# Part of the next image's sampling moved from the attention loop to the stage before it

## The chip, the cores and the metric

The kernel runs on one NeuronCore of a Trainium2 chip. A core has five engines that run side by side, each in the order of its own instructions: PE (TensorE, matrix products; its weight loads are listed apart as PEld), DVE (VectorE, elementwise work and reductions), ACT (ScalarE, activation functions), POOL (GpSimd, elementwise work and indirect transfers) and SP (SyncE, which issues most transfers). They wait for one another by semaphores. The metric is the device time of one execution in microseconds (us); the median of the runs shown is given, and less is better.

## The reference

The input is a batch of four images of 64 x 64 positions with 256 channels, that is 4096 tokens an image, all in float32. Two layers follow each other.

```
# layer 0: x = x + DCN(group_norm(x))
xp     = x @ in_w + in_b
x1     = silu(batch_norm(depthwise_conv3x3(x)))
offset = x1 @ off_w + off_b                     # 8 groups x 9 points x 2
mask   = softmax(x1 @ mask_w + mask_b over the 9 points)
out    = sum over points of mask * bilinear_sample(pad(xp), position + offset)
x      = x + out @ out_w + out_b

# layer 1, on tokens t of one image
v      = layer_norm(t)
q, k   = v @ Wt, v @ Wx.T                       # 32 units each
alpha  = sum_u tanh(q_u + k_u + bh_u) * Wa_u    # 4096 x 4096
t      = t + softmax(alpha) @ v
n      = layer_norm(t)
w      = n @ wr                                 # one weight a token
sel    = the 2047 tokens of largest w
y      = 0, but y[sel] = w[sel] * (gelu(n[sel] @ w1 + b1) @ w2 + b2)
t      = t + n + y
```

## The kernel before

The kernel works in stages. A first stage computes, for all four images, the projection `xp`, the offsets and the masks, and stores them. Then the sampling of image 0 runs alone. After that comes, for each image n, a *stage* and an *attention loop*. In the stage the feed-forward of image n-1 (`feed_forward`) and the attention preparation of image n (`attention_prep`) run interleaved. In the loop the attention of image n runs, and beside it the sampling of image n+1 (`sample_image`). Loop 3 has no sampling beside it. At the end the feed-forward of image 3 runs alone.

**The attention loop** (`attention`) has 8 query blocks by 32 key blocks, that is 256 tiles. The order of the work in a tile is written out by hand in four lists, one for each of ACT, PE, DVE and POOL (`order`), each entry with a lag in tiles, and `emit` issues them when what they need is done. In a tile PE makes six products `d` (line 869) and six products `nn` (line 879); ACT takes logarithm and exponential of three pairs of `d` (lines 951 and 953); DVE multiplies each of the six halves with its `nn` (line 884, entries `m1a` to `m3b`), POOL adds three of them (lines 957 and 959), DVE makes two more additions (lines 961 and 964), ACT the weight exponential (line 890). Every eight tiles give values to add up by eight products a tile on PE (line 906, `gather_values`); DVE adds them to the sums (`hand_over`). There are two PSUM buffers for `d`, three for `nn`, and one, "pm", for the values and for everything that the sampling needs from PE; `S.bank` says whether it is free.

**The sampling** (`sample_image`) is a Python generator: each `next` emits one step. First `list_tokens` makes the list of the tokens whose offsets are larger than one (32 one-hot comparisons at line 548, each with a product on PE). Then, for each of four chunks of 1024 positions and two channel halves, come 25 window positions. Each loads 512 KB of weights `wb` (line 673, on SP), multiplies (line 682, writing `prd`) and, but for the first, adds (line 689); each of the two is one step. So an image has 200 multiplications and 192 additions. After a chunk, four output steps each make four products with `outwp` (line 701), two DVE additions (lines 705 and 708) and a store. `wb` has two buffers in the loops. `single` is a second generator inside it, `exact_rows`, which gathers the listed tokens' samples exactly by 144 indirect transfers on POOL (line 616) and multiplies and reduces them on DVE (lines 627 and 628); it is advanced by one step after every multiplication.

In the loop the sampling is advanced by the entry `side`, which stands twice in DVE's list, so two steps a tile, until it is exhausted:

```
[("m1a", 1), ("m1b", 1), ("m2a", 1), ("side", 0), ("s3b", 2), ("side", 1), ("m2b", 1), ("sum", 2),
 ("m3a", 1), ("m3b", 1), ("out", 3)],
```

**The stage** advances its two generators by a string of turns, `m` for the feed-forward and `o` for the preparation. The feed-forward finds the threshold of the 2047 largest weights digit by digit (`kth_largest`), writes the rows in order of selection to DRAM by 32 indirect transfers on POOL (`sort<-v`, line 1253), stores the normalised rows (`base`, line 1266 on ACT, the store on SP), and then works through four groups of 512 rows: row load `xs` (line 1277, SP), normalisation on ACT (1286), transposes on PE and eviction `xT` on DVE (763, 764), hidden layer on PE (1302) and gelu on ACT, output layer on PE (1307), addition on DVE into `vs`, indirect store on POOL (1314). The preparation loads and normalises the tokens and then goes through eight *units*: transposes and eviction `vT`, products `pq` (795), threshold at zero `mm` (802), products `pk` and `pf` (810, 816), two exponentials on ACT (811, 818), the minimum `least` on DVE (828), a store of the query factor on SP (819).

Instructions that go through `keep` hold the order in which they are emitted; `pinned` does that for all DVE instructions of a function. The others are placed by a scheduler. Tiles come from pools; the names in `scope` give pool, buffers a tag, and whether it lies in PSUM.

Of the kernel before, what the change touches and what calls it, by code (L numbers as in the profile page):

```python
# [16 lines left out]
P = 128  # L17
# [14 lines left out]
CH = 1024  # L32
U = 32
# [11 lines left out]
def layers_kernel(ctx: ExitStack, tc: tile.TileContext, a, out: bass.AP):  # L45
# [185 lines left out]
    S = SimpleNamespace(bank=True, wants=False)  # L231
# [298 lines left out]
    def list_tokens(n):  # L530
# [22 lines left out]
        uf = S.two.tile([P, 1], F32, tag="uf", name="uf")  # L553
# [5 lines left out]
    def exact_rows(n, uf, out_rows):  # L559

        ui = S.two.tile([P, 1], I32, tag="ui", name="ui")
        nc.vector.tensor_copy(ui, uf)
        rf = S.two.tile([P, 1], F32, tag="rf", name="rf")
        nc.vector.tensor_scalar(rf, uf, float(L - 1), None, ALU.min)
        ri = S.two.tile([P, 4], I32, tag="rii", name="rii")
# [5 lines left out]
        hw = S.two.tile([P, 2], F32, tag="hw", name="hw")  # L571
# [72 lines left out]
        tt = S.sb.tile([P, C], F32, tag="tte", name="tte")  # L644
# [9 lines left out]
    def sample_image(n, depth=1):  # L654
# [8 lines left out]
        for c in range(L // CH):  # L663
            ac = S.dn.tile([P, CC, CH], F32, tag="ac", name="ac", bufs=min(depth, 2))
            for f in range(CC):
# [5 lines left out]
                for d in range(ND):  # L671
# [14 lines left out]
                    next(single, None)  # L686
# [4 lines left out]
            for i in range(0, CH // P, 2):  # L691
                while bank_taken():
                    next(single, None)
                    yield
# [22 lines left out]
    def sample_any(n):  # L717

        num = nc.values_load(large[0:1, n : n + 1], min_val=0, max_val=L)
        with tc.If(num > P), scope(  # L720
            ("two", 2, 0), ("sb", 2, 0), ("dn", 1, 0), ("ps_t", 1, 1), ("ps_m", 1, 1)
# [44 lines left out]
    def attention_prep(n, v, kf, vec):  # L766
# [33 lines left out]
        def below_zero(s):  # L800
            mms[s] = S.sb.tile([P, 512], F32, tag="mm", name="mm")
            vec.tensor_scalar(mms[s], pqs.pop(s), bqk, 0.0, ALU.add, ALU.min)

        def products(s):
# [14 lines left out]
            nc.sync.dma_start(out=qf_d[n][:, :, o], in_=qe)  # L819
# [4 lines left out]
        for s in range(8):  # L824
            if s < 7:
                units(s + 1)
            products(s)
            vec.tensor_reduce(least[:, s : s + 1], pks.pop(s).rearrange("p b q -> p (b q)"), AX.X, ALU.min)
            if s < 7:
                below_zero(s + 1)  # L830
            yield
# [12 lines left out]
    def attention(n, v, kf, beside):  # L844
# [94 lines left out]
        nb = NQ * NT  # L939
        rs, ds, ns = {}, {}, {}  # L940

        def emit(op, b):
# [31 lines left out]
            elif op == "side":  # L974
                for side in beside:
                    next(side, None)
# [5 lines left out]
            [("m1a", 1), ("m1b", 1), ("m2a", 1), ("side", 0), ("s3b", 2), ("side", 1), ("m2b", 1), ("sum", 2),  # L982
# [219 lines left out]
    def feed_forward(n, vec):  # L1202
# [60 lines left out]
        for i in range(NT):  # L1263
            if i % 4 == 0:
                base = S.sb.tile([P, 4, C], F32, tag="base", name="base")
            nc.scalar.activation(  # L1266
                base[:, i % 4, :], v[:, i, :C], AF.Identity, bias=nm[:, i : i + 1], scale=r1[:, i : i + 1]
            )
            if i % 4 == 3:
                nc.sync.dma_start(  # L1270
                    out=out_d[n, (i - 3) * P : (i + 1) * P].rearrange("(t p) c -> p t c", p=P), in_=base
                )
        yield
        hT2 = S.one.tile([P, 2, FF // P, 512], F32, tag="big", name="hT")
        for s in range(NSORT // 512):
            xs = S.row.tile([P, 4, C + 4], F32, tag="xs", name="xs")
            get = nc.sync.dma_start(  # L1277
# [26 lines left out]
            for t in range(4):  # L1304
# [12 lines left out]
                )  # L1317

# [18 lines left out]
    with scope(("two", 2, 0), ("sb", 2, 0), ("dn", 1, 0), ("ps_m", 2, 1)):  # L1337
# [3 lines left out]
    for n in range(NB):  # L1341
        with scope(("att", 1, 0)):
            v = S.att.tile([P, NT, C + 1], F32, name="v")
            kf = S.att.tile([P, 2, L], F32, name="kf")
            with scope(
# [3 lines left out]
                if n == 0:  # L1349
                    for _ in attention_prep(n, v, kf, nc.vector):  # L1350
                        pass
                else:


                    main, other = feed_forward(n - 1, pinned), attention_prep(n, v, kf, pinned)
                    for turn in "ommm" + "mo" * 5 + "moooo" + "moooo" + "m" + "mo" * 4:
                        next(main if turn == "m" else other, None)
                    for rest in (main, other):
                        for _ in rest:
                            pass  # L1360
            with scope(
                ("two", 2, 0), ("sb", 2, 0), ("dn", 1, 0), ("rp", 6, 0), ("qp", 2, 0),
                ("ep", 2 * PVB + 1, 0), ("ap", 1, 0), ("ps_d", 2, 1), ("ps_n", 3, 1), ("ps_m", 1, 1),
            ):
                attention(n, v, kf, [sample_image(n + 1)] if n + 1 < NB else [])
# [42 lines left out]
```

## Time and profile before

| | us |
|---|---|
| median of 3 runs | 11087.07 (11078.03 to 11089.36) |
| the profiled execution | 11100.44, span 11098.7 |
| PE busy in the span | 9437.4 (85%) |
| DVE busy | 8666.5 (78%) |
| ACT busy | 7403.1 (67%) |
| POOL busy | 5060.5 (46%) |
| mean granted PE clock | 0.896 |

The page lists the costliest groups of instructions: line, engine, operation, written and read tiles, form and count, then the busy time in us with the mean of one in ns, and the engine's idle time ahead of them with what ended most of it. The rows of the loop and of the sampling:

```profile
L879 PE MATMUL nn<-qn,kf 32*128 32x512 f32 (+1 forms) x12288 | 4727.3, 656 | 317.0 <-DVE r L884 272.6
L884 DVE TENSOR_TENSOR r<-nn,r 128x512 f32<-128x512 f32 x6144 | 3941.4, 682 | 1036.1 <-PE nn L879 1012.6
L957 POOL TENSOR_TENSOR r<-r 128x1024 f32<-128x1024 f32 x1024 | 2722.5, 2659 | 3347.2 <-DVE r L884 3345.0
L951 ACT ACTIVATE r<-d 128x1024 f32<-128x1024 f32 x3072 | 3120.4, 1016 | 1648.2 <-DVE r L961 1042.3
...
L689 DVE TENSOR_TENSOR ac<-ac,prd 128x1024 f32<-128x1024 f32 x768 | 1008.6, 1313 | 6.2
L682 DVE TENSOR_TENSOR prd<-xs,wb 128x1024 f32<-128x1024 f32 x768 | 984.2, 1282 | 0.0
L616 POOL DMA_INDIRECT ga<-tab,tii x576 | 731.8, 1270 | 241.3 <-issue 121.3
```

Each row sums over all four images. An average over the span mixes the loops with the stages between them, whose busy engines are not the same; windows of the span, each with the busy time of every engine in it, keep them apart. In the span, stage 0 lies at 1475 to 1569 us, loop 0 from there to 3730, the second stage to 4054, loop 1 to 6211, the third stage to 6522, loop 2 to 8679, the fourth stage to 8986, loop 3 to 10870, and the last feed-forward to the end.

### The profile page before, as it was taken

Reading aid. Unit: us, or ns where it says so; the run is one execution under the profiler, and the core shown is the slowest. Engines: PE = TensorE matmul, PEld = TensorE weight load, DVE = VectorE, ACT = ScalarE, POOL = GpSimd, SP = SyncE. Lnnn points to the kernel's source line nnn. Section 1 sums busy time; section 2 is a strip of 40 time slices with the busy share of each in tenths; the row PEclk is TensorE's granted clock in tenths of the full one; section 3 lists DMA queues with packets and bytes.
Section 4 is the critical chain, followed back from the end, with each engine's and each line's share of the span. In section 5 each row is a group of like instructions: output and inputs, shape, how many; then the busy total and the mean of one; then the engine's idle time right before and its main releaser. Section 6 shows DMA issues by size and latency. Waiting matters only on the chain. (4 is left out here: it accounts for less than half of the span.)

```text
span 11098.7 us, 116284 instructions
## 1 busy us (share of the span) xinstructions
PE 9437.4 (85%) x38460; PEld 4569.9 (41%) x38460; DVE 8666.5 (78%) x13502; ACT 7403.1 (67%) x8395; POOL 5060.5 (46%) x2931
## 2 busy tenths in 40 slices
PE   7870059999999689999999689999999699999996
PEld 4540024444444344444444344444444344444444
DVE  7767879898998549899998559899997457777772
ACT  4440037777878547777878457777878478888882
POOL 0005126654445337654545336654545245555552
PEclk9985569899999889899999889899999899999998
DMA  3336633222221223222220223322220200000002
GB/s 114 122 129 197 215 103 76 67 73 66 75 72 33 82 60 76 67 76 67 71 72 28 86 62 77 66 72 71 71 73 20 89 19 6 9 9 7 7 5 73
DMA packets 380819, 766.01 MB, mean 69 GB/s; under 512 B 48592, under 2 KB 212080, under 8 KB 380176
## 3 DMA queue, kind: packets, MB, share of 16 engines
q1 hardware_dynamic: 350032, 712.34, 19.8%
q0 software_dynamic: 30144, 45.87, 2.9%
q8 instruction: 309, 5.06, 0.2%
q14 instruction: 334, 2.74, 0.1%
HBM read 580.88 MB, written 177.14 MB: 68 GB/s over the span
## 5 line engine op out<-in xcount | busy, mean ns | idle before, releaser
L879 PE MATMUL nn<-qn,kf 32*128 32x512 f32 (+1 forms) x12288 | 4727.3, 656 | 317.0 <-DVE r L884 272.6
L884 DVE TENSOR_TENSOR r<-nn,r 128x512 f32<-128x512 f32 x6144 | 3941.4, 682 | 1036.1 <-PE nn L879 1012.6
L957 POOL TENSOR_TENSOR r<-r 128x1024 f32<-128x1024 f32 x1024 | 2722.5, 2659 | 3347.2 <-DVE r L884 3345.0
L951 ACT ACTIVATE r<-d 128x1024 f32<-128x1024 f32 x3072 | 3120.4, 1016 | 1648.2 <-DVE r L961 1042.3
L869 PE MATMUL d<-qf,kf 32*128 32x512 f32 (+1 forms) x12288 | 3431.6, 647 | 57.3 <-ACT r L951 49.3
L953 ACT ACTIVATE r<-r 128x1024 f32<-128x1024 f32 x3072 | 3125.3, 1051 | 32.6
L879 PEld LDWEIGHTS nn<-qn,kf 32*128 32x128 f32 (+1 forms) x12288 | 1456.7, 189 | 2196.5 <-DVE r L884 1755.7
L906 PE MATMUL pv<-v,et 128*128 128x257 f32 x8192 | 2258.8, 422 | 14.9 <-DVE acv L926 14.9
L906 PEld LDWEIGHTS pv<-v,et 128*128 128x128 f32 x8192 | 1606.2, 206 | 1079.2 <-issue 835.1
L869 PEld LDWEIGHTS d<-qf,kf 32*128 32x128 f32 (+1 forms) x12288 | 1034.0, 189 | 1328.1 <-issue 636.0
L959 POOL TENSOR_TENSOR r<-r 128x512 f32<-128x512 f32 x1024 | 1322.5, 1292 | 163.5 <-DVE r L884 88.9
L689 DVE TENSOR_TENSOR ac<-ac,prd 128x1024 f32<-128x1024 f32 x768 | 1008.6, 1313 | 6.2
L682 DVE TENSOR_TENSOR prd<-xs,wb 128x1024 f32<-128x1024 f32 x768 | 984.2, 1282 | 0.0
L616 POOL DMA_INDIRECT ga<-tab,tii x576 | 731.8, 1270 | 241.3 <-issue 121.3
L890 ACT ACTIVATE et<-et,nshift 128x512 f32<-128x512 f32 x1024 | 725.3, 708 | 25.1 <-DVE et L964 25.1
L961 DVE TENSOR_TENSOR r<-r 128x512 f32<-128x512 f32 x1024 | 712.4, 696 | 13.3 <-POOL r L957 12.9
L964 DVE TENSOR_TENSOR et<-r 128x512 f32<-128x512 f32 x1024 | 696.1, 680 | 6.0 <-POOL r L959 5.6
L701 PE MATMUL pmo<-outwp,ac 128*128 128x256 f32 x512 | 138.9, 421 | 455.7 <-DVE ac L689 407.6
L115 ACT ACT_TABLE_LOAD x9 | 11.5, 1283 | 768.6 <-DVE mv L743 681.8
L476 POOL MEMSET w<- 128x1600 f32 x16 | 22.9, 1433 | 675.1 <-PE ptw L493 388.1
L701 PEld LDWEIGHTS pmo<-outwp,ac 128*128 128x128 f32 x512 | 100.9, 206 | 513.0 <-DVE ac L689 284.8
L416 PE MATMUL pc<-xn,diag 128*128 128x512 f32 x576 | 263.0, 611 | 33.4 <-ACT xn L362 33.4
(354 smaller groups left out, 5211.1 us busy)
## 6 DMA issues: line engine op xcount, KB each, us to landing
wb<-wt SPq DMA_DIRECT2D x800, 512.0 KB
tab<-tb SPq DMA_DIRECT2D x128, 256.0 KB
v<-t SPq DMA_DIRECT2D x64, 512.0 KB
xs<-xp SPq DMA_DIRECT2D x32, 680.0 KB
xp<-xp SPq DMA_DIRECT2D x32, 544.0 KB
xt<-in_x_dram SPq DMA_DIRECT2D x32, 512.0 KB
xr<-in_x_dram SPq DMA_DIRECT2D x64, 256.0 KB
t<-xr SPq DMA_DIRECT2D x64, 256.0 KB
```

The source lines that it names most:

```text
L616: keep(nc.gpsimd.indirect_dma_start(out=ga[:, s, dy].rearrange("p c e -> p (c e)"), out_offset=None, in_=tab_d[n], in_offset=bass.Indirect ...
L682: keep(nc.vector.tensor_tensor(pr.rearrange("p (r w) -> p r w", w=W), src, wb.rearrange("p (r w) -> p r w", w=W), ALU.mult,))
L689: keep(nc.vector.tensor_add(ac[:, f, :], ac[:, f, :], pr))
L869: keep(nc.tensor.matmul(d[:, j, :], kf[g, blk, rows(kt)], qs[q][0][g, blk, :], start=True, stop=True))
L879: keep(nc.tensor.matmul(nn, kf[g, blk, rows(kt)], qs[q][1][g, blk, :], start=True, stop=True))
L884: keep(nc.vector.tensor_tensor(r[:, j, :], ns[j], r[:, j, :], ALU.mult))
L890: keep(nc.scalar.activation(ets[b], ets[b], AF.Exp, bias=nshift))
L906: keep(nc.tensor.matmul(pv, ets[b0 + i][:, rows(j)], v[:, k0 + i, :], start=(i == 0), stop=(i == PVB - 1)))
L951: keep(nc.scalar.activation(rs[b, p], ds.pop((b, p)), AF.Ln))
L953: keep(nc.scalar.activation(rs[b, p], rs[b, p], AF.Exp, scale=-1.0))
L957: keep(nc.gpsimd.tensor_tensor(rs[b, 1], rs[b, 1], rs[b, 2], ALU.add))
L959: keep(nc.gpsimd.tensor_tensor(rs[b, 1][:, 0], rs[b, 1][:, 0], rs[b, 3][:, 0], ALU.add))
```

## The change

The sampling of image n+1 is begun in the stage before loop n. The string of turns gets a third letter, `s`, for one step of sampling. Stage 0 takes 26 such steps, the later stages 122; what is left goes on in the loop. There one step a tile is taken, and a second one (`again`) in as many tiles as the rest of 412 steps needs: 130 of 256 in loop 0, 34 in loops 1 and 2. While the stage runs, `S.gather` is false, and the multiplications don't advance the exact rows.

So that both fit and don't queue behind one another, other things change. The sampling's small tiles get a pool `smp`, and `dn` now lives over stage and loop. `mm` has one buffer instead of two. `base` holds two row blocks instead of four, with three buffers, and is stored from ACT's queue; the query factors too. The row loads `xs` are issued on POOL instead of SP. The feed-forward yields after each of the first three output products of a group, the preparation twice more in each unit, so that steps can be set between them. Stage 0 runs the preparation pinned.

```diff
@@
-    S = SimpleNamespace(bank=True, wants=False)
+    S = SimpleNamespace(bank=True, wants=False, gather=True)
@@ sample_image
-                    next(single, None)
+                    if S.gather:
+                        next(single, None)
                     yield
@@ attention_prep
-            mms[s] = S.sb.tile([P, 512], F32, tag="mm", name="mm")
+            mms[s] = S.sb.tile([P, 512], F32, tag="mm", name="mm", bufs=1)
...
-            nc.sync.dma_start(out=qf_d[n][:, :, o], in_=qe)
+            nc.scalar.dma_start(out=qf_d[n][:, :, o], in_=qe)
...
             if s < 7:
                 units(s + 1)
+            yield
             products(s)
             vec.tensor_reduce(least[:, s : s + 1], pks.pop(s).rearrange("p b q -> p (b q)"), AX.X, ALU.min)
+            yield
             if s < 7:
                 below_zero(s + 1)
             yield
@@ attention
-    def attention(n, v, kf, beside):
+    def attention(n, v, kf, beside, steps):
...
+        second = min(max(steps - nb, 0), nb)
...
-            elif op == "side":
+            elif op == "side" or op == "again" and (b + 1) * second // nb > b * second // nb:
                 for side in beside:
                     next(side, None)
...
-            [("m1a", 1), ("m1b", 1), ("m2a", 1), ("side", 0), ("s3b", 2), ("side", 1), ("m2b", 1), ("sum", 2),
+            [("m1a", 1), ("m1b", 1), ("m2a", 1), ("side", 0), ("s3b", 2), ("again", 1), ("m2b", 1), ("sum", 2),
@@ feed_forward
-            if i % 4 == 0:
-                base = S.sb.tile([P, 4, C], F32, tag="base", name="base")
+            if i % 2 == 0:
+                base = S.sb.tile([P, 2, C], F32, tag="base", name="base", bufs=3)
...
-                nc.sync.dma_start(
-                    out=out_d[n, (i - 3) * P : (i + 1) * P].rearrange("(t p) c -> p t c", p=P), in_=base
+                nc.scalar.dma_start(
+                    out=out_d[n, (i - 1) * P : (i + 1) * P].rearrange("(t p) c -> p t c", p=P), in_=base
...
-            get = nc.sync.dma_start(
+            get = nc.gpsimd.dma_start(
                 out=xs, in_=sort_d[n][s * 512 : (s + 1) * 512].rearrange("(t p) c -> p t c", p=P)
...
+                if t < 3:
+                    yield
@@ layers_kernel
-        with scope(("att", 1, 0)):
+        with scope(("att", 1, 0), ("smp", 2, 0), ("dn", 1, 0)):
...
+            sampling = sample_image(n + 1) if n + 1 < NB else iter(())
+            S.gather = False
...
-                    for turn in "ommm" + "mo" * 5 + "moooo" + "moooo" + "m" + "mo" * 4:
-                        next(main if turn == "m" else other, None)
+                main = feed_forward(n - 1, pinned) if n else iter(())
+                prep = attention_prep(n, v, kf, pinned)
+                if n:
+                    turns = "ommm" + "mo" * 5 + "moooo" + "mss" + "oss" * 12 + "m" + ("ossss" * 3 + "msss" * 4) * 4
+                else:
+                    turns = "o" * 10 + "ss" + "os" * 24
+                for turn in turns:
+                    next({"m": main, "o": prep, "s": sampling}[turn], None)
...
+            S.gather = True
...
-                attention(n, v, kf, [sample_image(n + 1)] if n + 1 < NB else [])
+                attention(n, v, kf, [sampling], STEPS - turns.count("s") if n + 1 < NB else 0)
```

`STEPS` is 412.

## The prediction

> **What bounds the kernel now.** I read the page's slices first, then a window for each stage and loop, then the waits inside the loops, then the stage by time. The slices say where to cut:
>
> ```profile
> DVE  7767879898998549899998559899997457777772
> ...
> PEclk9985569899999889899999889899999899999998
> ```
>
> The first three attention loops have VectorE (DVE) at 8 to 9 tenths, the fourth at 7; between loops DVE falls to 4 or 5. The windows put sizes on that (us, busy time and instructions of PE, weight loads, DVE, ACT, POOL, then granted clock, DMA share, GB/s):
>
> ```profile
> 1475.00:1569.00 94.00, 62.47 (x161) 26.77 (x162) 41.64 (x95) 34.57 (x51) 0.16 (x1) 0.76 0.28 95
> 1569.00:3730.00 2161.00, 2036.83 (x8370) 943.06 (x8371) 1938.00 (x2891) 1655.85 (x1794) 1195.66 (x659) 0.93 0.22 63
> 3730.00:4054.00 324.00, 215.37 (x672) 128.84 (x670) 98.31 (x310) 100.44 (x147) 57.48 (x53) 0.77 0.30 96
> 4054.00:6211.00 2157.00, 2032.74 (x8354) 937.80 (x8355) 1933.11 (x2864) 1653.83 (x1792) 1197.16 (x659) 0.94 0.22 63
> 8986.00:10870.00 1884.00, 1814.91 (x8176) 829.75 (x8173) 1374.10 (x2371) 1667.00 (x1792) 1010.92 (x512) 0.97 0.02 7
> ```
>
> Rows: stage 0, loop 0, the stage before loop 1, loop 1, loop 3. A loop with sampling is 2157 to 2161 us, the loop without is 1884: sampling costs 275 us a loop, and adds 1933 - 1374 = 559 us of DVE work. The stage of 324 us uses DVE for 98.
>
> ```profile
> 2800.00:2960.00 160.00, 158.26 (x666) 72.55 (x666) 159.37 (x220) 134.46 (x147) 83.28 (x43) 0.99 0.23 73
> 9100.00:9200.00 100.00, 99.30 (x464) 45.31 (x462) 73.36 (x123) 93.75 (x101) 57.81 (x29) 1.00 0.00 1
> ```
>
> Two undisturbed stretches, 32 matmuls a tile: with two sampling steps a tile DVE is full and a tile takes 160 / (666/32) = 7.7 us; without sampling PE is full and it takes 100 / (464/32) = 6.9 us. The waits say the same; first 2340:3440 of loop 0, then 9010:10840 of loop 3:
>
> ```profile
> DVE r L884 <- PE nn L879: 61.1, 64, 2.8
> ...
> DVE r L884 <- PE nn L879: 475.4, 454, 4.1
> ```
>
> DVE hardly waits for PE while it samples, and waits 475 us when it doesn't. So DVE bounds the sampled tiles, PE the rest. In loop 0 sampling ends at 3440 of 3730: the load is also uneven.
>
> **What the Trainium skill says.** "Perfetto Trace Analysis", Optimization Strategy: where regimes have different most-contended engines, interleaving them may help. The windows are such a case: DVE 90% in the loop, 30% in the stage. "VectorE: DVE Perf Modes", the perf-mode tier table: a float32 tensor_tensor runs at 1x only, 2293 ns for 2048 elements; half of that agrees with the 1.21 us of the 1024-element steps, so only their place can change. "TensorE: Matmul & The Clock Gate", Part 1: an idle PE falls to half clock. The trace agrees: matmuls of 587 ns and of 1220 ns, and a clock of 0.77 in the stage; longer holes in the stage cost twice. "DMA: Bandwidth & Descriptors", Issuing engines are not separate DMA queues: moving a DMA to another issuer saves sequencer time only. The trace shows it as queueing on SP, not as speed.
>
> **The change part by part.** I counted instructions in the built order of both kernels. Loops 1 and 2: the stage takes 61 of 200 multiplications, 57 of 192 additions, 4 output pairs and the token list; 139 and 135 stay in the loop, 4 output pairs fall behind its last product. Loop 0: 14 and 12 go to stage 0, 6 and 7 with 4 pairs fall behind the loop.
>
> Loops 1 and 2. Leaving: 118 steps by 1.30 us (rows of L682 and L689) = 153, 8 output pairs by 1.38 = 11, the list about 14 (32 by 0.286, and its small operations). DVE 1933 - 178 = 1755 us, 6.86 a tile. DVE was 93.5% busy at best over a long stretch (4800:5920, 1047 of 1120), so alone it would set 6.86 / 0.935 = 7.33 us a tile. PE alone sets loop 3's pitch, 7.26 (1851.5 us between the first and last weight exponentials, over 255). Both are almost equal; no row shows two engines this near together. Below: 7.26, since PE's work is not reduced. Above: 7.9, nearly today's 8.2 (1120 us for 136 tiles). I take 7.5, 2.5% over the slower one. Window: 1884 + 256 x 0.24 = 1945, that is -212 each. This includes the start: today the list and the row preparation stand ahead of loop 1's first quotients, and its first exponential comes 57 us after the last product of the stage (4034.6 to 4091.4) against 29 in loop 3.
>
> Loop 0: leaving 39 steps by 1.30 = 51, 4 pairs 6, the list 14; DVE 1938 - 71 = 1867, 7.29 a tile, over 0.935 is 7.8; I take 7.85. Window 1884 + 256 x 0.59 = 2035, -126. Loop 3 has no sampling: 0.
>
> Gathers (144 by 1.27 us on POOL an image) now come with every second tile instead of every tile. POOL had 6.2 us of work in an 8.9 us tile while gathering (512 of 730 us); spread out, its cover stays: 0.
>
> Tails: after loops 1 and 2 four output pairs run through one PSUM buffer, about 2.5 us each (four 0.38 us matmuls, a 0.69 us addition, the handshakes), and their store must land before the next token load, which heads SP's queue: 15 each. Loop 0 also has 13 steps by 1.2: 32. Sum +62.
>
> The stage, which can be hurt. DVE runs in order, so each step delays what is behind it.
>
> ```profile
> 3831.49 0.96 POOL L1253 DMA_INDIRECT sort<-v,rif  x1 [0.31 <-issue]
> ...
> 3863.93 1.23 DVE L255 COPY xT<-ptt 128x1024 f32<-128x1024 f32 x1 [1.83 <-PE ptt L763]
> ...
> 3901.44 1.23 DVE L255 COPY xT<-ptt 128x1024 f32<-128x1024 f32 x1 [3.84 <-PE ptt L763]
> ...
> 3948.71 1.23 DVE L255 COPY xT<-ptt 128x1024 f32<-128x1024 f32 x1 [3.81 <-PE ptt L763]
> ```
>
> The row gather rw is now behind the 32 sort scatters on POOL (the last ends at 3832.5), and DVE's preparation behind it: DVE stands until about 3837. Then come 16 small operations (3), 4 minima, 3 copies, 4 thresholds (12) and 22 sampling steps by 1.2 (26) before the first xT: about 3879 instead of 3864, +15. In the four feed-forward groups the first gets a unit of preparation ahead of its hidden-layer products (37.5 becomes 50: +12); the other three have 12 to 15 steps and 3 us of preparation ahead of the first output product, about 25 us against 28 us that PE needs, so hidden; then three steps between output products make their pitch 4.1 against 3.45 (+2), and the row load issued on POOL behind the last scatter adds 2.5: 3 x 4.5 = 13. Output pairs in the last group: +8. The unit and list work that today follows the last group is gone: -10. Sum 38; I take 45 for load stalls. Stage 0 gets 26 steps (31) and the list (12) into 52 us of DVE idleness in a PE chain: 25. With the stage before loop 3 and the last feed-forward, which sample nothing but take the moved DMAs (base stores and query stores on ACT, row loads on POOL): +15, bounds -20 and +40, since ACT's 11.0 us of idleness before the query exponential at 3837, which ended just after SP's row load, may go, but ACT now issues 24 DMAs.
>
> Do the loads follow?
>
> ```profile
> 1702.43 1.22 DVE L682 TENSOR_TENSOR prd<-xs,wb 128x1024 f32<-128x1024 f32 x1
> ...
> 1703.68 0.51 SPq L673 DMA_DIRECT2D wb<-wt  x1
> ...
> 1705.50:1706.50 1.00, 1.00 (x6) 0.58 (x4) 1.00 (x3) 0.97 (x3) 1.00 (x1) 1.00 0.61 246
> 1706.50:1707.50 1.00, 1.00 (x6) 0.31 (x6) 1.00 (x3) 1.00 (x2) 0.92 (x2) 1.00 0.68 279
> ```
>
> A multiplication frees its buffer at 1703.65, SP issues at once, the bytes have moved by about 1707.3: 3.6 us. With two buffers and pairs back to back (2.4 us) the next use of that buffer starts 3.6 us after it was freed: it just fits. Bounds of a stage's growth: +10 and +110.
>
> Sum: -212 - 212 - 126 + 62 + 45 + 45 + 25 + 15 = -358. The profiled execution took 11100.4 (span 11098.7); the median is 13 lower. 11100 - 358 - 13 = 10729: 10730.
>
> **The rivals.**
> A: two nearly full engines in lock step. The ring of three nn buffers lets PE run only one pair ahead, so a step inside the products stalls PE; sampled tiles stay at 7.9, in loop 0 at 8.05. For it: PE loses clock after holes (0.94 in loop 1, 0.97 in loop 3). Against: at 2800:2960 a full DVE leaves the clock at 0.99. Loops -109, -109, -75; sum -101: 10985.
> B: the stage hides the steps, the loops reach PE's floor: 7.3 and 7.6, stages +20, +20, +15, +5 for the rest. For it: 226 us of idle DVE a stage. Against: the order above. -263, -263, -190, +122 = -594: 10495.
> C, slower: the stage is paced by its mask loads. Each of the 61 multiplications then adds its whole load turnaround to the stage, since DVE waits in order and the feed-forward's evictions stand behind. Without the two stages' growth the change gains 448, so it decides at 224 / 61 = 3.7 us a multiplication; at 5 us (3.6 and 1.2 of its own, under contention) it is 2 x 305 - 448 = +162: 11250. Against: DMA share is 0.1 in the groups.
> That the change doesn't move the steps is excluded by the counts.
>
> **How the numbers follow.** Forecast 0.66, A 0.12, B 0.17, C 0.05. The likeliest alone lies in 10600 to 10880. The range 10490 to 10990 leaves out half of A and of B and all of C, about 0.19. This kernel's measurement tells 0.2%, 22 us, from no change: faster 0.93, same 0.02 (the far end of A), slower 0.05 (C).
>
> **What would show it.** Loops 1 and 2 near 1945 us and loop 0 near 2035, with PE 95% busy and DVE's wait for nn between 61 and 475; stages at 355 to 370 us with DVE above 240 us busy; multiplications in the groups waiting little for wb; the first xT about 150 us after the loop's last product, 134 before. Wrong, if the loops stay above 2050, or a stage exceeds 435.

## The result and the profile after

The changed kernel takes 10886.27 us (median of 4 runs, 10878.54 to 10899.14), the kernel before 11088.22 in the same session: a ratio of 0.9818, 95% interval 0.9801 to 0.9835, 202 us saved. The forecast was 10730, with a range of 10490 to 10990: the sign and the range held, but 156 us of the 358 expected did not come. The profiled execution has a span of 10897.4 us, 201.3 less than before, and can be cut into the same stretches. Here a loop runs from its first `d` product to the start of its last `pv` product, for both kernels, and a stage is what lies between two loops. A loop's tail, the steps and output pairs that are left over behind it, is counted to the stage:

| stretch | before | after | difference | forecast |
|---|---|---|---|---|
| up to loop 0 | 1569.4 | 1580.6 | +11 | +25 |
| loop 0 | 2166.9 | 2075.2 | -92 | -126 |
| stage before loop 1, with loop 0's tail | 317.8 | 425.7 | +108 | +77 |
| loop 1 | 2157.2 | 1983.8 | -173 | -212 |
| stage before loop 2, with loop 1's tail | 311.2 | 401.3 | +90 | +60 |
| loop 2 | 2156.3 | 1988.1 | -168 | -212 |
| stage before loop 3, with loop 2's tail | 306.9 | 329.1 | +22 | +30 |
| loop 3 and last feed-forward | 2113.0 | 2113.6 | +1 | 0 |

So the loops gave 117 us less than forecast, the stages with sampling took 61 more, while stage 0 and the stage before loop 3 were 22 better than assumed (the 15 us that the prediction put down for all of the rest are counted to that stage here). The windows of the changed kernel: loop 0, a stage with sampling, loop 1, the stage without, loop 3 (us, busy time and instructions of PE, weight loads, DVE, ACT, POOL, then granted clock, DMA share, GB/s):

```profile
1580.60:3655.80 2075.20, 1954.26 (x8294) 913.44 (x8294) 1858.62 (x2775) 1648.63 (x1792) 1182.61 (x657) 0.94 0.22 60
3655.80:4081.50 425.70, 256.91 (x740) 151.47 (x738) 267.33 (x488) 99.37 (x144) 70.08 (x62) 0.70 0.50 163
4081.50:6065.30 1983.80, 1882.72 (x8262) 869.22 (x8262) 1747.30 (x2689) 1646.49 (x1792) 1158.22 (x654) 0.96 0.18 50
8454.70:8783.80 329.10, 219.47 (x644) 124.34 (x643) 94.36 (x272) 101.02 (x146) 61.22 (x58) 0.76 0.27 92
8783.80:10672.60 1888.80, 1820.07 (x8191) 834.11 (x8192) 1376.54 (x2377) 1666.70 (x1792) 1008.39 (x513) 0.97 0.02 7
```

DVE's work went where the counts said: 1747 us in loop 1 (1755 forecast), 267 in the stage, which had 98. PE is busy 94.9% of loop 1. Yet loop 1 is 95 us longer than loop 3, where the forecast had 61. The waits inside loop 1 (4150 to 6040; who waited for whom, us, times, longest):

```profile
PEld nn L888 <- DVE r L893: 359.4, 523, 3.1
...
DVE r L893 <- PE nn L888: 196.6, 366, 3.4
...
PE nn L888 <- DVE r L893: 56.7, 40, 2.3
```

DVE and PE now wait for each other. DVE's wait lies between the 61 and 475 us that the prediction named; how the loop divides into tiles bound by one and by the other shows only tile by tile. I took a tile as the time between two weight exponentials (L890 before, L899 after), called what it takes beyond 6.95 us its excess, and sorted the tiles by what DVE begins in them besides the attention's own operations. Loop 1, and loop 3 for comparison (number of tiles, mean us, sum of the excess in us):

| tiles with | loop 1 before | loop 1 after | loop 3 after |
|---|---|---|---|
| no step | 26, 6.78, -4 | 21, 6.82, -3 | 193, 6.95, -1 |
| one step | none | 120, 7.14, +23 | none |
| two or three steps | 140, 7.90, +133 | 42, 7.37, +18 | none |
| an output pair | 26, 8.85, +50 | 10, 9.56, +26 | none |
| the sum of gathered rows | 7, 11.04, +29 | 7, 10.75, +27 | none |
| the exact rows' product | 1, 11.83, +5 | 1, 13.66, +7 | none |
| the end of a query block | 55, 9.13, +120 | 54, 8.33, +75 | 62, 8.20, +78 |

By this table 160 of the 173 us that loop 1 gained lie in its tiles; the rest lies ahead of them, where the list no longer stands. The median tile of loop 1 fell from 7.60 to 6.96 us, and that is loop 3's median (6.95). Of the 120 plain one-step tiles 90 take at most 7.0: most steps cost nothing at all. What is left above loop 3 is in few places: 60 us in 18 tiles in which DVE has a larger piece of other work. One of them, DVE first and PE after it (start, duration, engine, operation, idle time before it and what ended it):

```profile
4223.70 1.21 DVE L684 TENSOR_TENSOR prd<-xs,wb 128x1024 f32<-128x1024 f32 x1
4224.83 1.35 DVE L629 TENSOR_TENSOR ga<-ga,wg 128x1152 f32<-128x1152 f32 x1
4226.21 2.10 DVE L630 TENSOR_REDUCE so<-ga 128x32 f32<-128x1152 f32 x1
4228.23 0.68 DVE L971 TENSOR_TENSOR r<-r 128x512 f32<-128x512 f32 x1
...
4230.10 0.70 PE L878 MATMUL d<-qf,kf 32*128 32x512 f32 x2 [2.47 <-ACT r L961]
4230.63 0.59 PE L878 MATMUL d<-qf,kf 32*128 32x512 f32 x2
...
4232.90 1.22 PE L878 MATMUL d<-qf,kf 32*128 32x512 f32 x2
```

4.7 us of DVE stand ahead of the attention's addition L971; ACT's logarithm waits for it, PE for ACT, and 2.8 us after PE comes back its products take 1.22 us instead of 0.59: the granted clock is 0.50 from 4233 to 4236, after the hole. The tile takes 10.34 us, the next 8.83.

### The profile page after: what moved, and what is told of

It is laid out like the page before. It is cut to its first block, busy times and chain, and to the rows that moved or that the text cites. A ratio compares the mean times of both kernels' runs of the same rounds, so it can differ in the third digit from the quotient of the medians.

```text
span 10897.4 us, 115889 instructions
## 1 busy us (share of the span) xinstructions
PE 9186.4 (84%) x38460; PEld 4477.6 (41%) x38460; DVE 8586.7 (79%) x13502; ACT 7381.2 (68%) x8388; POOL 5001.3 (46%) x2947
## 5 line engine op out<-in xcount | busy, mean ns | idle before, releaser
L888 PE MATMUL nn<-qn,kf 32*128 32x512 f32 (+1 forms) x12288 | 4486.1, 646 | 281.1 <-DVE r L893 243.3
L878 PE MATMUL d<-qf,kf 32*128 32x512 f32 (+1 forms) x12288 | 3376.3, 638 | 63.7 <-ACT r L961 59.4
L888 PEld LDWEIGHTS nn<-qn,kf 32*128 32x128 f32 (+1 forms) x12288 | 1398.8, 188 | 2008.3 <-DVE r L893 1530.7
L692 DVE TENSOR_TENSOR ac<-ac,prd 128x1024 f32<-128x1024 f32 x768 | 968.2, 1261 | 9.4
L684 DVE TENSOR_TENSOR prd<-xs,wb 128x1024 f32<-128x1024 f32 x768 | 954.0, 1242 | 20.9 <-DMA wb<-wt 18.8
L618 POOL DMA_INDIRECT ga<-tab,tii x576 | 660.6, 1147 | 223.8 <-issue 118.6
L899 ACT ACTIVATE et<-et,nshift 128x512 f32<-128x512 f32 x1024 | 723.7, 707 | 26.6 <-DVE et L974 26.6
L971 DVE TENSOR_TENSOR r<-r 128x512 f32<-128x512 f32 x1024 | 699.9, 684 | 2.7 <-POOL r L967 2.6
L1324 POOL DMA_INDIRECT out_dram<-vs,si x64 | 74.6, 1165 | 563.3 <-DVE vs L257 386.5
```

The source lines that it names most:

```text
L684: keep(nc.vector.tensor_tensor(pr.rearrange("p (r w) -> p r w", w=W), src, wb.rearrange("p (r w) -> p r w", w=W), ALU.mult,))
L692: keep(nc.vector.tensor_add(ac[:, f, :], ac[:, f, :], pr))
L878: keep(nc.tensor.matmul(d[:, j, :], kf[g, blk, rows(kt)], qs[q][0][g, blk, :], start=True, stop=True))
L888: keep(nc.tensor.matmul(nn, kf[g, blk, rows(kt)], qs[q][1][g, blk, :], start=True, stop=True))
L899: keep(nc.scalar.activation(ets[b], ets[b], AF.Exp, bias=nshift))
L971: keep(nc.vector.tensor_add(rs[b, 1][:, 1], rs[b, 1][:, 1], rs[b, 3][:, 1]))
```

## The experiments

Theory 1 holds that each tile stands for itself and takes the longer of PE's and DVE's time. Its rival, theory 2, is the forecast's own reading, that the loop follows DVE's sum over a mean share. Theories 3 to 5 are about the stage. The times are medians of 4 runs, with the ratio to the kernel before, run on the same chip, and its interval; loops and stages come from one profiled execution each. To compare: the changed kernel's 0.9818.

The runs were made on four chips, here called 5, 7, 9 and 11; on which chip the kernel before and the changed kernel were traced is not on record. The end of this section shows a stall in the stages that is in all traces from chips 5 and 9, and in those of the kernel before and the changed kernel, but in none from chips 7 and 11. It is worth 20 to 25 us in each of two stages. Loops don't have it and can be compared throughout; stages, and whole times, only with this in mind.

**Two steps in every tile, same work.**

```diff
-        second = min(max(steps - nb, 0), nb)
+        second = nb
```

> The changed kernel with one edit: the loop takes two sampling steps in every tile until the steps are used up, as before the change; the stage keeps its steps. DVE's work in a loop is the same. Theory 1, each tile stands for itself: a tile takes the longer of PE's 6.95 us and DVE's 5.05 us plus 1.26 for each step, so one step is free and a second costs about 0.65 (0.9 where PE's clock suffers). Then some 137 tiles have two steps instead of 34, and the end has 119 without: loops 1 and 2 grow by 60 to 90 us, loop 0 by 15 to 40; the tails after the loops (about 60 us in all) go, as the steps end earlier. Sum about +75 to +160 on 10886: 10960 to 11050. Theory 2, the forecast's reading, the loop follows DVE's sum over its mean share of 0.935: loops unchanged within 15 us, only the tails go, 10810 to 10850.

11053.96 us on chip 5, 0.9956 (0.9940 to 0.9973). Loops 2136, 2068, 2071: +61, +84, +83; the stages 37, 17 and 26 shorter, as the tails went. The tails brought DVE 20 us of work into loops 1 and 2, and 29 into loop 0; the rest of the growth, some 60 us in loops 1 and 2, comes from the pacing alone, where theory 2 allowed 15. Theory 2 falls; theory 1 holds for loops 1 and 2 and was too low for loop 0, so that its sum just misses. The gathers, which come twice as often here, are not the reason: the median tile with two steps takes 7.60 us while they run and 7.60 after them. Sixteen undisturbed tiles with two steps, in the columns of the windows above:

```profile
5061.10:5182.70 121.60, 120.82 (x515) 55.24 (x512) 121.47 (x169) 102.51 (x113) 63.33 (x33) 1.00 0.23 72
```

The same view of six tiles with one step each in the changed kernel:

```profile
5207.50:5249.20 41.70, 41.43 (x192) 19.05 (x192) 38.22 (x59) 38.53 (x44) 28.93 (x19) 1.00 0.19 43
```

121.60 / 16 = 7.60 us with DVE full (121.47); 41.70 / 6 = 6.95 with PE full and DVE at 38.22. Both at a clock of 1.00: the one kind of tile is bound by DVE, the other by PE. Between tiles with one step a tile with two costs somewhat less, 7.37 in the table above, so tiles do not stand for themselves entirely.

**No sampling in the stages**: the turns `s` are struck out, and the steps go to the loops.

```diff
+                turns = turns.replace("s", "")
                 for turn in turns:
```

> The changed kernel with no sampling in the stages: the whole of it in the loops, 256 first steps and 156 second ones spread evenly; the moved DMAs stay. It shows what the even pacing gives without the stage. Theory 1 (each tile for itself): against the changed kernel 122 more second steps a loop at 0.65 (79 us), four more output pairs inside (26), the list and row preparation back at the loop's start (28), so loops 1 and 2 near 2110 us against 1984; the stages come down by about 75 to 90 us to near 330. Sum some +80 to +140: 10965 to 11025. Rival: the stage is where the gain is and pacing brings nothing; then the loops stay at 2157 and the time is 11080 to 11130 with the moved DMAs.

11009.49 on chip 5, 0.9918 (0.9902 to 0.9935). Loops 2102, 2100, 2100, stages 344, 344, 338: inside theory 1's range. Even pacing takes 57 to 65 us off each loop without the stage's help and gives some 32 a stage back as a tail, by which the first sort scatter of the stage comes later. Together with the small edits that stay, it carries some 45% of the gain (0.82% of 1.82%).

**The groups of the feed-forward without steps.**

```diff
-turns = ... + ("ossss" * 3 + "msss" * 4) * 4
+turns = ... + ("o" * 3 + "m" * 4) * 4
```

> The changed kernel with the sampling steps taken out of the four feed-forward groups of a stage (96 turns); the list and 24 steps ahead of the first group stay. The 96 go to the loop as second steps. From the runs so far: a group takes 45 to 46 us with no steps and 53 to 59 with them, so the stages of loops 1 and 2 shorten by 35 to 45 us each; in the loop a second step costs 0.65 us in a plain tile and about 1.2 in one that has other work on DVE, so loops 1 and 2 grow by 70 to 100 us each. Sum +50 to +120 us on the changed kernel. Rival: the groups' growth is that of the moved DMAs and the steps are hidden there; then the stages hardly shorten and the sum is +130 to +200.

11013.50 on chip 9, 0.9931 (0.9914 to 0.9947). The times of the transposed rows xT, one for each group, in the stage before loop 2 of the changed kernel, from the timeline of DVE (start, duration, operation, idle time before it):

```profile
6238.57 1.21 DVE L257 COPY xT<-ptt 128x1024 f32<-128x1024 f32 x1
6297.29 1.22 DVE L257 COPY xT<-ptt 128x1024 f32<-128x1024 f32 x1 [3.45 <-PE ptt L767]
6352.03 1.23 DVE L257 COPY xT<-ptt 128x1024 f32<-128x1024 f32 x1 [3.41 <-PE ptt L767]
6407.09 1.23 DVE L257 COPY xT<-ptt 128x1024 f32<-128x1024 f32 x1 [4.92 <-PE ptt L767]
```

And in the kernel with free groups:

```profile
6300.67 1.21 DVE L257 COPY xT<-ptt 128x1024 f32<-128x1024 f32 x1
6352.91 1.23 DVE L257 COPY xT<-ptt 128x1024 f32<-128x1024 f32 x1 [3.45 <-PE ptt L767]
6401.30 1.23 DVE L257 COPY xT<-ptt 128x1024 f32<-128x1024 f32 x1 [3.41 <-PE ptt L767]
6447.62 1.23 DVE L257 COPY xT<-ptt 128x1024 f32<-128x1024 f32 x1 [4.92 <-PE ptt L767]
```

A group goes from 59, 55, 55 us to 52, 48, 46, and the last from its xT to its last addition from 49 to 35. From their first scatter on, the stages before loops 1 and 2 are 40 and 41 us shorter; loops 1 and 2 are 89 and 82 longer, and the tails behind them 20 each. For 96 steps that is 0.4 us each in the stage and 0.9 in the loop, or 1.1 with the tail, output pairs included: the steps are not hidden in the groups, but cheaper there. The sum, +127 us, lies just above its range, which had no longer tails.

**The steps' tails back beside the last tiles**: `STEPS = 436`.

> The changed kernel with the planned count of sampling turns raised from 412 to 436, so that the loop's pacing has 24 more second steps and the steps are used up some tiles before the loop's end: the tail (four output pairs, in loop 0 also 13 steps) moves back beside the last tiles. It prices the tails alone. Theory 1: the stages shorten by what the tails cost, 35 + 15 + 20 us; each loop grows by 24 second steps less the pairs' cover, 15 to 22 us; sum -25 to +5 us on the changed kernel. Rival: the tail costs little because the stage's load of the tokens has to wait for the last attention rows anyway; then stages shorten by less than 15 us in all and the sum is +30 to +60.

10937.45 on chip 11, 0.9866 (0.9850 to 0.9883). The first sort scatter comes 56.6, 57.2 and 55.7 us after the loop's last product instead of 90.3, 67.5 and 69.8 (55.8, 55.6 and 55.7 before the change). So the tails cost 34, 10 and 14 us, 58 in all, where the forecast had 62. But the loops grow by 39, 54 and 50: in loop 1 the pairs' tiles rise from 26 to 43 us of excess, the query blocks' ends from 75 to 99, the plain tiles from 38 to 52. Theory 1 had the price of a second step from plain tiles only. That the time falls in the rival's range is luck: this trace is without the stall, and the list takes 18 us in its stages instead of 50. Against an estimate of the changed kernel without the stall, 10843 us (the last run of this section), the growth is some 90 us, outside both ranges.

**The sum of the gathered rows in two tiles.**

```diff
             keep(nc.vector.tensor_tensor(gf, gf, wv.to_broadcast([P, 4 * K2, CG]), ALU.mult))
+            yield
             keep(nc.vector.tensor_reduce(
```

> The changed kernel with one more turn between the weighting of eight gathered groups (1.35 us on DVE) and their reduction (2.10 us), so that they no longer stand in one tile behind a sampling multiplication. DVE's work is the same. Theory 1 (each tile for itself): the seven or eight such tiles of a loop take 10.7 us and the next about 8.9; split, they take about 7.7 and 8.4: some 2.5 to 3.5 us less for each, 20 to 28 a loop in three loops, -60 to -85 us in all. Rival (the loop follows DVE's sum): no change within 12 us.

10844.43 on chip 11, 0.9785 (0.9769 to 0.9802), but not as theory 1 had it: loops 1 and 2 are 1991.8 and 1991.9, no shorter than 1983.8 and 1988.1. The four tiles from a weighting on have 51 us of excess over the loop, 59 in the changed kernel, and other tiles take that back. In a tile whose slack is 0.6 us, 1.35 us too much and later 2.1 us too much cost about what 3.45 in one piece does. Loop 0 gained 15 us, and the stages 29, 24 and 6: the list of tokens in them took 25 us instead of 50, which nothing in the edit asks for. This trace too is without the stall, and against the estimate of 10843 us for the changed kernel without it nothing is gained, which is the rival's figure.

**The list out of the stage**, back to the loop's start:

```diff
-        uf = yield from list_tokens(n)
-        yield
         exact = []
-        single = exact_rows(n, uf, exact)
+        def listed_rows():
+            uf = yield from list_tokens(n)
+            yield
+            yield from exact_rows(n, uf, exact)
+        single = listed_rows()
```

> The changed kernel with the token list (32 DVE comparisons, each followed by PE products, then the row preparation) taken out of the stage and put back to the start of the loop, where it was before the change; the stage keeps its 118 steps. Theory 3, the list is what delays the stage's start: the first transposed rows xT come 20 to 40 us sooner after the first sort scatter (107 us now, 72 before), the stage of loop 1 falls from 426 to about 395, while each loop starts about 28 us later: time 10865 to 10930. Rival, the sampling steps and the mask loads delay it: xT moves by less than 10 us, and the time rises by the loops' later starts, 10940 to 10980.

10918.13 on chip 5, 0.9834 (0.9818 to 0.9851). The first xT comes 94 us after the first scatter, 107 in the changed kernel, 82 in the stages without list and steps and 72 before the change. So the list is worth 13 us there and the steps ahead of the first group 12; 10 are neither's. These are no clean prices: all four traces have the stall, in this kernel and in the one without list and steps not at the list but at another operation, with 21 to 24 us. The move is less than theory 3 asked and more than the rival allowed.

**The list as the first turn of the stage**:

```diff
-turns = "ommm" + "mo" * 5 + "moooo" + "mss" + "oss" * 12 + ...
+turns = "s" + "ommm" + "mo" * 5 + "moooo" + "ms" + "oss" * 12 + ...
```

> The changed kernel with the token list as the stage's first turn, ahead of the selection of the k largest, instead of after the sort scatters were issued. Theory 3, the list is dear where it stands because in the scatters' time each comparison and product pair takes up to 5.6 us: the first xT comes 8 to 15 us sooner after the first scatter (107 us now), the first scatter is later by no more than 5 us; -10 to -30 us in all. Rival, the list costs its own DVE and PE time wherever it stands: the first scatter is 12 to 25 us later and the sum is -5 to +25.

10875.91 on chip 11, 0.9813 (0.9797 to 0.9830): by the time alone no difference that can be told. xT comes 82 us after the first scatter, 24 sooner, and the first scatter 16 us later, since the selection now waits for the list, which takes 15 us instead of 50. But this trace is without the stall. Without it the list takes no more than 26 us in its old place too, and xT comes 90 us after the first scatter (the last run of this section); so the list's new place brings xT some 7 us and costs the scatter 16, and against the estimate of 10843 us the time is some 30 longer. That is the rival's side.

**The moved DMAs back on SP.**

```diff
-            nc.scalar.dma_start(out=qf_d[n][:, :, o], in_=qe)
+            nc.sync.dma_start(out=qf_d[n][:, :, o], in_=qe)
...
-                nc.scalar.dma_start(
+                nc.sync.dma_start(
...
-            get = nc.gpsimd.dma_start(
+            get = nc.sync.dma_start(
```

> The changed kernel with the three moved DMAs given back to SP: the base stores and query stores from ACT, the row loads from POOL. Forecast's term: the moves cost 15 us in the stage without sampling. Theory 4: in the stage before loop 3, which has no sampling, the time falls by 5 to 15 us (329 now), but in the stages of loops 1 and 2 row loads and query stores now stand on SP behind mask loads that wait for a buffer, so that these grow by 10 to 60 us each: 10890 to 11000. Rival: SP is never in the way, and the time falls by 20 to 45 us in all three stages: 10840 to 10870.

10877.57 on chip 5, 0.9800 (0.9784 to 0.9816). The stages are 10, 3 and 10 us shorter than in the changed kernel's trace, the loops equal within 4, and neither range held. The 10 us before loop 3 look like theory 4's 5 to 15, but three other kernels on chip 5 keep the moved DMAs, and from its first scatter on this stage takes 247 to 248 us in them, 250 here and 259 in the changed kernel's trace alone. The stages before loops 1 and 2, with sampling, likewise take 331 and 327 in the kernel with two steps a tile and 328 and 331 here. So no cost of the moves shows, without sampling or with it, and SP's queue behind the mask loads (`wb`) did no harm either, against theory 4. Nor are the mask loads a brake: in the changed kernel's stage before loop 2 DVE's waits for them are few (who waited for whom, us, times, longest):

```profile
DVE si L257 <- DMA xs<-sort: 24.7, 3, 10.0
...
DVE prd L684 <- DMA wb<-wt: 9.4, 11, 2.4
```

**Combinations.** The moved DMAs on SP, 436 turns and the split sum:

> The changed kernel with the three moved DMAs back on SP, 436 turns and the split sum together. If the gains add: -20 for the DMAs, -20 to 0 for the tails, -60 to -85 for the sum: -80 to -120 us on the changed kernel, some 10770 to 10810. If the split sum doesn't help (rival of that run): -20 to -40.

10893.24 on chip 11, 0.9822 (0.9806 to 0.9838): the gains don't add; the longer loops of the 436 turns came along. They are 10, 13 and 16 us shorter than with the 436 turns alone, so beside more second steps the split sum seems to help. The split sum and the DMAs on SP alone:

> The changed kernel with the split sum and the three DMAs back on SP. If the two gains add (42 and 18 us): 10815 to 10835 us. If the first came from the place of the list in the instruction stream rather than from the tiles it sits in, moving other DMAs may bring the list's 50 us back, and it is 10850 to 10885.

10868.86 on chip 9, 0.9797 (0.9781 to 0.9814): the second case by its numbers, as the list takes 50 us again in both stages. That the moved DMAs brought them back is not shown; the chip is another one than the split sum's, and has the stall. The same with the list first and `"oss" * 24` instead of `"os" * 24` in stage 0, at the same pacing of loop 0:

> As the last one, with the list as the stage's first turn and 24 more sampling steps in stage 0 in place of loop 0's tail of 13 steps. Stage 0 longer by 10 to 20 us, the tail after loop 0 shorter by 25 to 35, the list's stall out of the scatters' time for good, the first scatter 17 us later: 10790 to 10830; if the steps in stage 0 aren't covered there, 10820 to 10860.

10878.70 on chip 9, 0.9801 (0.9784 to 0.9817), outside both ranges. The list takes 15 us, and the tail after loop 0 is some 30 shorter. But the 24 further steps lengthened the way to loop 0 by 35 us, more than their own time: stage 0's idle time was used up by the change's 26. And loop 0, with the tail's steps back in it, is 30 us longer, which no forecast had.

**The list's stall.** Its 32 comparisons on DVE alternate with products on PE. In the changed kernel some of them in the stage before loop 1 look like this, and so do some in the next stage ("remote": the trace names no engine of the core as what ended the wait):

```profile
3772.36 0.29 DVE L550 TENSOR_SCALAR oh<-slotr,bf 128x128 f32<-128x128 f32 x1 [5.33 <-remote]
3777.99 0.29 DVE L550 TENSOR_SCALAR oh<-slotr,bf 128x128 f32<-128x128 f32 x1 [5.34 <-remote]
3783.59 0.29 DVE L550 TENSOR_SCALAR oh<-slotr,bf 128x128 f32<-128x128 f32 x1 [5.31 <-remote]
```

To see whether the place in the instruction streams matters, unused instructions were set ahead of the first stage:

```diff
...
+        for _ in range(96):
+            keep(nc.vector.memset(spare_row, 0.0))
+            keep(nc.scalar.activation(other_row, tok[:, 0, :], AF.Identity))
+            keep(nc.tensor.matmul(spare_ps, ones, tok[:, 0, :], start=True, stop=True))
```

> The changed kernel with 96 small instructions each on DVE (memset of 128x2), ACT (copy of 128x2) and PE (a 128x2 product) ahead of the first stage; they compute nothing that is used and cost 10 to 30 us there. Everything behind them is the same, 96 places later in each engine's instruction stream. The list takes 50 us in the stages of loops 1 and 2 in the changed kernel and in four of its variants, 17 to 25 in two others that have the same list beside the same scatters. Theory 5, the list's stall hangs on the position in the instruction streams: in at least one of the two stages the list takes 15 to 35 us or over 60, and the first xT moves by 10 us or more from +107. Rival, it hangs on the work beside it: 48 to 52 us and +105 to +108 in both. Time: 10870 to 10920 in either case.

10865.10 on chip 7, 0.9801 (0.9785 to 0.9818). The list takes 26 and 25 us, xT comes 90 and 89 us after the first scatter, and the stages are 25, 21 and 10 us shorter, while the added instructions cost 22 ahead of loop 0. The list's own row in each kernel (count, shortest, median and longest ns, first and last start) with the idle time ahead of it, in the stage before loop 1; the changed kernel:

```profile
L550 DVE TENSOR_SCALAR oh<-slotr,bf x32: 189/286/425, 3746.1 to 3796.3; 128x128 f32<-128x128 f32 x32
...
  remote: 25.9, 5
```

The kernel with the unused instructions:

```profile
L550 DVE TENSOR_SCALAR oh<-slotr,bf x32: 266/286/454, 3767.8 to 3793.9; 128x128 f32<-128x128 f32 x32
...
  PE pl L551: 3.5, 11
```

The comparisons are as long as before; the 26 us of waits are gone. Theory 5 foretold that, but the run doesn't show theory 5, because the chip has changed with the position. In all traces, the waits of DVE and ACT that end by "remote" sum to this, in the stages before loops 1, 2 and 3:

| chip | kernel | us |
|---|---|---|
| not on record | before | 17, 18, 19 |
| not on record | changed | 26, 26, 38 |
| 5 | two steps in every tile | 29, 26, 42 |
| 5 | no sampling in the stages | 21, 22, 41 |
| 5 | list in the loop | 24, 22, 42 |
| 5 | DMAs back on SP | 42, 29, 11 |
| 9 | groups without steps | 9, 18, 36 |
| 9 | split sum and DMAs | 19, 44, 9 |
| 9 | the same, list first | 29, 24, 24 |
| 11 | 436 turns; split sum; list first; all three | none in any stage |
| 7 | unused instructions | none in any stage |

The stage before loop 3 has no list and no sampling, and its waits too come on chips 5 and 9 and stay away on 7 and 11. There they are at other operations, as with two steps in every tile (who waited, us, times, longest):

```profile
DVE mm L257 <- remote: 21.8, 2, 13.8
...
ACT qe L822 <- remote: 15.1, 1, 15.1
```

The split sum alone and with the DMAs on SP has as many instructions of PE and of DVE ahead of the list in its trace, and takes 26 us for it on chip 11 and 50 on chip 9. In the five kernels without such waits the list takes 15 to 26 us. So whether there is a stall goes with the chip, or with something else that differed between these sessions. Whether the position has any part in it is not shown.

The kernel with the unused instructions, less their 22 us, can stand for the changed kernel without the stall: 10843 us, an estimate, 43 less than measured. No run is faster than that, although those on chips 5 and 9 carry the stall; no edit here is shown to be better than the change as it stands.

## Why the prediction was right, and where it was short

- **Loops 1 and 2, the largest miss of the reading.** The term "both are almost equal ... I take 7.5, 2.5% over the slower one" was too good; measured 7.62 and 7.64 us a tile: 39 and 44 us. It divided DVE's sum by a mean share, and so blended tiles that have separate bounds. Plain tiles did better than it thought, most one-step tiles at PE's 6.95; the sums, pairs and products in 18 tiles did worse, at 9.6 to 13.7. That the two errors lie on opposite sides is luck. By the same reading even pacing alone would bring nothing; it carries some 45% of the gain.
- **Loop 0.** 7.85 was taken, 7.98 measured, for the same reason: 130 second steps. At 2075 us it is above the 2050 that the prediction set as its own mark for being wrong; loops 1 and 2 are below it.
- **Rival A**, the lock step, had a nearer time (10985 against 10886 measured), but its mechanism, a step that stalls PE in every sampled tile, is refuted by the 6.95 us tiles at a clock of 1.00.
- **Rival B**, loops at PE's floor and stages that hide the steps, is refuted: loop 1 is 95 us above loop 3, and the stages grew by 108 and 90.
- **Tails.** 62 forecast, 58 measured, by the first scatter.
- **The stage's start.** The term was +15: rw behind the scatters, and 22 steps. Measured from first scatter to xT: 72 us before, 107 and 106 after, +35 and +34. In the four traces without the stall that have the list in the same place it is 89 to 94, so some 17 us go with the stall; with them gone, the term would have been near. The sign "the first xT about 150 us after the loop's last product" failed: 197 and 173, of which the tails are 34 and 12, where 127 is the figure before. The stage itself, forecast at 355 to 370 us, came to 391 and 389 without its tail, and to 366 and 369 in the kernel with the unused instructions, without the stall. So most of what the stages took beyond the forecast is the stall's, as far as one run shows.
- **The groups.** For the stage before loop 2: first group +12 forecast, +20 measured; the other two +4.5 each, +11 each; the last +8, +10; the end -10, -8. For the stage before loop 1, whose lines the prediction shows: +22, +6, +8, +9, -7. The run with free groups shows that 5 to 9 us of a group and 13 to 15 of the last are the steps' doing. The forecast held most of them for hidden behind PE's products; which of them are not, no run tells.
- **Stage 0.** +25 forecast, +11 measured, and +9 to +20 in the other runs that have the same stage 0. DVE's idle time covered more than thought, but not 24 further steps.
- **Moved DMAs.** +15 for all of the rest, with bounds -20 and +40. The stage before loop 3 grew by 8 beyond its tail, but only in this trace: with the moves on chip 5 it is 3 to 4 us shorter than before, from the first scatter on. ACT's 11.0 us of idle time, which the prediction placed at SP's row load, end by "remote" in the trace, and are of the stall's kind.
- **Rival C** is refuted: the waits for masks in a stage sum to 9.4 us; it needed 3.7 for each of 61 multiplications.

The forecast leaned on the Trainium skill, "Perfetto Trace Analysis", Optimization Strategy, by which interleaving stretches that have different most-contended engines may help. That holds here, with a price: 0.4 us for a step in a stage against 0.9 in a loop whose slack is used up.

## What to carry to other kernels

Where two engines bound a loop by turns, price a helper's step tile by tile, as the longer of the two engines' times with the step added, and not from sums over the loop: here the first step of a tile was free and a second cost 0.65 us, or 0.9 with all that came with it. Spread such work evenly before looking for another place for it, and look for the few tiles in which it meets other work. Before a gain or loss of some 20 us is put down to an edit, check that it lies where the edit is, and that the two traces come from the same chip: here all four kernels on chip 11 lost a stall at once, whatever their edit.

## What was not expected of the hardware

In the stages DVE and ACT stand for some 5 us at a time, and up to 24 in one piece, until something ends the wait that the trace doesn't name. These stalls are in all 27 stages traced on chips 5 and 9 and in the first session, and in none of the 15 traced on chips 7 and 11, with five different kernels. At the list, which stands in DVE's way, they cost 20 to 25 us a stage (425.7 and 401.3 us in the changed kernel, 400.2 and 380.2 with the unused instructions). In the stage before loop 3 as much as 42 us of them cost nothing that shows: 248 us from the first scatter on with them, 250 with 436 turns without them. What ends these waits, and whether it is the chip or something else in the session, no run here tells. The kernel before had stalls of the same kind, at other operations; from the waits of its stage before loop 1 (who waited, us, times, longest):

```profile
ACT qe L818 <- remote: 11.0, 1, 11.0
DVE mm L255 <- remote: 5.7, 2, 5.0
```
